# Two engines share the copies of turned attention weights: another split in the third and the fourth batch element

## The chip, the cores and the metric

The kernel runs on one core of a Trainium2 chip. That core has five engines with instruction streams of their own: TensorE (PE, with its weight loads shown apart as PEld), VectorE (DVE), ScalarE (ACT), GpSimd (POOL) and SyncE (SP), whose stream issues the DMAs. Each stream is carried out in the order in which it was built; an instruction that waits for another engine holds up all that stand behind it in its own stream. The metric is the device time of one execution in microseconds (us), and the number to be predicted is the median of several runs.

## The reference

Four batch elements of 512 tokens with 512 channels pass through two blocks. Block 0 is a WKV recurrence over the context and a feed-forward layer (FFN) with quantised activations and one-bit weights. Block 1 is a cross-attention with 16 heads of 32 channels and a last layer with ternary weights. The attention is the part that matters here:

```python
q = _qdq(x) @ _qdq(wq).T + bq
kv = cond @ wkv.T + bkv
k, v = jnp.split(kv, 2, axis=-1)
...
attn = jax.nn.softmax(jnp.einsum('bnhd,bmhd->bhnm', q, k) * scale, axis=-1)
o = jnp.einsum('bhnm,bmhd->bnhd', attn, v).reshape(B, N, C)
out = _qdq(o) @ _qdq(wp).T + bp
```

`attn` must be turned (token axis against key axis) before it can be multiplied with `v` on TensorE. Each turned block appears in PSUM, the accumulators of TensorE, and is copied from there to SBUF, the working memory. The change is about who does that copy.

## The kernel before

The four elements, b = 0 to 3, run as a pipeline. While the FFN of element b+1 runs, the attention of element b fills the gaps, and the WKV part of b+2 beside it. All these parts are Python generators (`ffn_layer`, `attention_layer`, `ternary_layer` and others); `run` takes the next step of the one that is due first, by a place on a time axis that was written out by hand. That fixes TensorE's order through chained dependencies (`in_turn`, `next_turn`). The orders of VectorE and ScalarE are made at build time by a scheduler that estimates when each instruction could run, so moving one instruction from one engine to another can move its neighbours as well.

The attention of one element (`attention_layer`) has 16 units, k = 0 to 15: a unit is one pair of heads, i = 0 and 1, and one half of the queries, which is two tiles of 128, t = 0 and 1. Iteration k of its main loop does, on TensorE and in this order:

- `scores(k, i, 0)`: two score tiles `s_ps`. For each, VectorE takes the negated row maximum, `at_nm` (L962), and ScalarE the exponential, `at_P` (L964). These tiles share three PSUM buffers.
- `values(k-2)`: sixteen small matmuls into `o_ps` from the turned weights `at_PT` of unit k-2; ScalarE copies the result to `at_os` (L1004).
- `turned(k-1, i, 0)`: two groups of four transposes into `pt_ps`, each copied into `at_PT` (L982 by VectorE, L984 by ScalarE).
- `scores(k, i, 1)`, then `turned(k-1, i, 1)`, then `collect(k-2)`: `ot_ps`, divided into `at_o` by VectorE (L1022), with `at_rt` the reciprocal sums (L1020).

So a unit has four copies of turned weights. They are written (k, t, i) below. `at_PT` has one buffer, and `values` starts when all four of its unit are there. In the elements 0 to 2 `pt_ps` shares three PSUM buffers with `o_ps`, `ot_ps`, `qr_ps`, `sx_ps`, `q_ps`; in the fourth element, which the code calls `alone`, `pt_ps` has two buffers of its own, since no FFN runs any more.

```python
dst = PT[k][:, i, :, t * P : (t + 1) * P]
if alone and i:
    made[k] = nc.vector.tensor_copy(dst, blocks(pt))
else:
    made[k] = nc.scalar.copy(dst, blocks(pt))
```

Before its units, an element is prepared in halves of two token tiles. For the fourth element's second half (tiles 2 and 3) this falls among the last units of the third element, once the FFN has written those tiles (`xb`, L788). VectorE computes the layer norm: `BATCH_NORM_STATS2` (L225) and its aggregate (L228), `ln_v`, then about fifteen tiny instructions of a reciprocal square root (`rs_half`, `rs_y`, `rs_t`, L185 to L195), and `ln_r` (L237, L238). GpSimd centres the tiles (`at_xn`, L246), VectorE takes their maxima (`at_s`, L249) and scales (L259, L260), ScalarE rounds (`at_xn`, L264), TensorE turns them (`qr_ps`), ScalarE stores them (`at_xqT`, L271). Then `project(0)` makes the first queries: `q_ps` on TensorE, `at_q` (L912) and `at_half` (L917, L918), a DMA out to `qD` and four DMAs back to `at_qR`, which the first `scores` of the fourth element needs.

Among the first eight units of the fourth element lies the end of the third: `project_out` (`at_o` rounded by ScalarE, `p_ps`, then `at_y` L1058 and `xb` L1059 on VectorE) and the ternary layer, whose statistics, `tf_xn` (L1158) and `tf_s` (L1162 to L1176) are on VectorE, followed by ScalarE's rounding (`tf_xn`, L264), TensorE's `qr_ps` and `f_ps`, and the store (L1190).

Of the kernel before, what the change touches and what calls it, by code (L numbers as in the profile page):

```python
# [30 lines left out]
def kernel(  # L31
# [37 lines left out]
    NB, T, D = x.shape  # L69
# [63 lines left out]
    def psum_tile(name, tag, dtype=F32):  # L133
        pool, bufs = psum["now"]
        return pool.tile([P, D], dtype, name=name, tag=tag, bufs=bufs[tag])
# [34 lines left out]
    def transpose(*args):  # L170
        return in_turn(nc.tensor.transpose(*args))  # L171

    def blocks(a):
        return a.rearrange("p (c q) -> p c q", q=P)
# [680 lines left out]
    def attention_layer(b, xb, pool, tiles=range(NT)):  # L855
# [6 lines left out]
        alone = b == NB - 1  # L862
# [86 lines left out]
        units = [(p, h) for p in range(NP) for h in range(len(tiles) // 2)]  # L949
# [22 lines left out]
        def turned(k, i, t):  # L972

            if k not in PT:
                PT[k] = pool.tile([P, 2, NT, 2 * P], F32, name="at_PT", tag="at_PT", bufs=1)
            w = lanes.pop((k, i, t))
            pt = psum_tile("pt_ps", "acc" if alone else "m")
            for m in range(NT):
                transpose(pt[:, m * P : (m + 1) * P], w[:, m * P : (m + 1) * P], ident)
            dst = PT[k][:, i, :, t * P : (t + 1) * P]  # L980
            if alone and i:
                made[k] = nc.vector.tensor_copy(dst, blocks(pt))  # L982
            else:
                made[k] = nc.scalar.copy(dst, blocks(pt))  # L984
# [99 lines left out]
        for k in range(len(units) + 2):  # L1084
# [8 lines left out]
            for i in range(2):  # L1093
                if before:
                    turned(k - 1, i, 0)
# [8 lines left out]
            for i in range(2):  # L1104
                if before:
                    turned(k - 1, i, 1)
# [331 lines left out]
```

## Time and profile before

| what | value |
|---|---|
| runs | 1122.58, 1123.04, 1125.3 us; median 1123.04 |
| the profiled execution | 1121.98 us; its span 1120.2 us, so 1.78 us lie around the span |
| busy: PE, PEld | 960.3 us (86%), 678.2 us (61%) |
| busy: DVE, ACT, POOL | 886.3 us (79%), 711.5 us (64%), 297.8 us (27%) |
| mean granted TensorE clock | 0.954 |
| copies of turned weights | 224 on ACT, 32 on DVE |

Times inside the profile are microseconds from the start of the span. The shares are means over a pipeline whose stages have different limits; what matters here is the stretch from about 945 to 1040 us, where the third element's attention ends and the fourth's begins. A row of the timeline gives start, duration, engine, line, operation, the tile written and the tiles read, and, in brackets, how long the engine stood idle before it and what released it. VectorE and ScalarE instructions that follow each other overlap a little: two copies of 0.59 us on ACT that start one after the other take 1.07 us together.

### The profile page before, as it was taken

The page shows a single profiled execution, that of the slowest core. Times are in us where ns is not written, and L with a number is a line of the kernel's source. Part 1 is how long each engine was busy: PE and PEld are TensorE (multiplying, and loading weights), DVE is VectorE, ACT ScalarE, POOL GpSimd, SP SyncE. Part 2 cuts the span into 40 slices and gives each one's busy share as a digit, 9 for nine tenths or more (in the row PEclk, how much of TensorE's full clock was granted, in tenths as well). Part 3 has the DMA queues.
Part 4 walks back from the last instruction along what each step waited for, and adds up shares of the span by engine and source line. Part 5 has one row for each costly group of instructions (what it writes and reads, how often), then busy time and mean ns, then how long its engine had stood idle before and what let it go on. Part 6 is the DMA issues. An engine that isn't in the chain of part 4 may idle for free.

```text
span 1120.2 us, 16509 instructions
## 1 busy us (share of the span) xinstructions
PE 960.3 (86%) x5520; PEld 678.2 (61%) x5548; DVE 886.3 (79%) x1884; ACT 711.5 (64%) x1454; POOL 297.8 (27%) x301
## 2 busy tenths in 40 slices
PE   3879898978878978899998797999999899788983
PEld 3345565555546756677776475777777677555651
DVE  5887447778877799998759899977689766689866
ACT  5657655453214677667768676687676677887762
POOL 3822014333104143541215536212122400100000
PEclk8889999998888999999999999999999899999997
DMA  8188953544434664654655555464564563243401
GB/s 281 39 274 321 322 203 129 178 169 153 148 122 151 224 191 157 200 178 163 205 188 184 164 168 181 142 220 157 181 227 156 181 201 110 89 134 109 123 11 38
DMA packets 85668, 189.58 MB, mean 169 GB/s; under 512 B 12240, under 2 KB 36816, under 8 KB 74576
## 3 DMA queue, kind: packets, MB, share of 16 engines
q1 hardware_dynamic: 85584, 188.53, 50.2%
q8 instruction: 44, 0.72, 0.3%
q14 instruction: 40, 0.33, 0.1%
HBM read 148.65 MB, written 39.85 MB: 168 GB/s over the span
## 4 chain that ended last, share of the span: by engine, by line
PE 46%; DVE 28%; ACT 12%; issue 5%; DMA 5%; POOL 3%; SPq 1%; POOLq 0%; ACTq 0%; DVEq 0%
PE ff_hp L168 13%; PE ff_acc L168 6%; PE pt_ps L171 6%; PE o_ps L168 4%; PE v_ps L168 3%; PE s_ps L168 3%; DVE wk_q L655 3%; DVE at_nm L962 3%; ACT at_P L964 3%; PE k_ps L168 2%; PE tp_ps L171 2%; DVE qg_i L695 2%; PE qr_ps L171 1%; ACT at_PT L984 1%; DVE ff_z L765 1%
## 5 line engine op out<-in xcount | busy, mean ns | idle before, releaser
L168 PE MATMUL ff_hp<-wT,xp 128*128 128x512 f32 x1024 | 270.5, 408 | 3.3 <-ACT at_P L964 2.1
L168 PEld LDWEIGHTS ff_hp<-wT,xp 128*128 128x128 f32 x1024 | 194.3, 193 | 51.3 <-ACT at_P L964 4.4
L964 ACT ACTIVATE at_P<-s_ps,at_nm 128x512 f32<-128x512 f32 x256 | 174.5, 689 | 61.8 <-DVE at_nm L962 61.4
L962 DVE TENSOR_REDUCE at_nm<-s_ps 128x1 f32<-128x512 f32 x256 | 166.0, 677 | 28.4 <-PE s_ps L168 28.0
L700 POOL TENSOR_TENSOR ff_z<-qg_b,qg_s 128x512 f32<-128x512 bf16 x64 | 71.1, 1111 | 381.1 <-ACT qg_b L699 328.4
L171 PE MATMUL pt_ps<-ident,at_P 128*128 128x128 f32 x1024 | 141.3, 278 | 11.7 <-ACT at_os L1004 5.2
L984 ACT COPY at_PT<-pt_ps 128x512 f32<-128x512 f32 x224 | 124.7, 595 | 38.1 <-PE pt_ps L171 37.5
L171 PEld LDWEIGHTS pt_ps<-ident,at_P 128*128 128x128 f32 x1024 | 113.2, 141 | 53.1 <-issue 13.8
L168 PE MATMUL ff_acc<-wT,hr 128*128 128x512 f32 x512 | 136.6, 408 | 6.3 <-DVE hr L712 3.3
L168 PE MATMUL s_ps<-at_kR,at_qR 128*128 128x512 f32 x256 | 98.1, 449 | 21.9 <-ACT at_P L964 14.6
L168 PEld LDWEIGHTS ff_acc<-wT,hr 128*128 128x128 f32 x512 | 92.4, 190 | 27.3 <-DVE hr L712 4.6
L760 ACT ACTIVATE ff_z<-ff_hp,coef 128x512 f32<-128x512 f32 x64 | 43.9, 686 | 67.2 <-PE ff_hp L168 65.2
L168 PE MATMUL o_ps<-at_PT,at_V 128*32 128x256 f32 x1024 | 72.0, 395 | 1.3 <-DVE hr L712 0.7
L699 ACT CAST qg_b<-qg_i 128x512 bf16<-128x512 int8 x80 | 49.4, 618 | 36.7 <-DVE qg_i L695 24.6
L168 PE MATMUL v_ps<-wkvT,cT 128*128 128x512 f32 x128 | 65.9, 664 | 5.3 <-DVE wT L336 2.3
L765 DVE SCALAR_TENSOR_TENSOR ff_z<-ff_hp,coef,ff_z 128x512 f32<-128x512 f32 x64 | 47.6, 744 | 27.9 <-PE ff_hp L168 27.8
L168 PEld LDWEIGHTS s_ps<-at_kR,at_qR 128*128 128x128 f32 x256 | 45.7, 193 | 39.4 <-ACT at_P L964 23.8
L761 DVE SCALAR_TENSOR_TENSOR ff_z<-ff_z,ff_hp 128x512 f32<-128x512 f32 x64 | 43.4, 679 | 24.2 <-ACT ff_z L760 24.0
L168 PE MATMUL k_ps<-cT,wkvT 128*128 128x512 f32 x128 | 59.3, 613 | 3.1 <-ACT cT L479 1.4
L711 ACT CAST hr<-tp_ps 128x512 fp32r<-128x512 f32 x64 | 37.6, 587 | 35.7 <-PE tp_ps L171 35.7
L655 DVE RECIPROCAL wk_q<-wk_q 128x256 f32<-128x256 f32 x32 | 54.3, 1718 | 1.4 <-POOL wk_p L643 1.4
L171 PE MATMUL tp_ps<-ident,ff_z 128*128 128x128 f32 x256 | 41.2, 286 | 14.4 <-ACT at_PT L984 5.3
(190 smaller groups left out, 1735.7 us busy)
## 6 DMA issues: line engine op xcount, KB each, us to landing
wT<-wD SPq DMA_DIRECT2D x72, 1024.0 KB, 5.2
wn<-in_L_ffn_w_dram SPq DMA_DIRECT2D x18, 1024.0 KB, 6.8
at_kR<-kD SPq DMA_DIRECT2D x128, 128.0 KB, 3.0
at_qR<-qD SPq DMA_DIRECT2D x256, 64.0 KB, 2.2
wD<-wT SPq DMA_DIRECT2D x12, 1024.0 KB, 5.0
kD<-k_half SPq DMA_DIRECT2D x16, 512.0 KB, 3.3
qD<-at_half SPq DMA_DIRECT2D x32, 256.0 KB, 2.1
cn<-in_ctx_dram SPq DMA_DIRECT2D x8, 512.0 KB, 5.9
```

Of the source, the lines that this page charges most:

```text
L168: return in_turn(nc.tensor.matmul(*args, **kwargs))
L171: return in_turn(nc.tensor.transpose(*args))
L655: nc.vector.reciprocal(half, half)
L699: nc.scalar.copy(qb, qi)
L700: nc.gpsimd.tensor_tensor(grouped(src), grouped(qb), s.unsqueeze(2).to_broadcast([P, NG, GS]), ALU.mult)
L711: nc.scalar.copy(part[:, 0, :], pt)
L760: nc.scalar.activation(z, hp, AF.Tanh, scale=coef[:, 0:1])
L761: nc.vector.scalar_tensor_tensor(z, z, 1.0, hp, ALU.add, ALU.mult)
L765: nc.vector.scalar_tensor_tensor(z, hp, coef[:, 1:2], z, ALU.mult, ALU.mult)
L962: nc.vector.tensor_reduce(nm, sp, AX.X, ALU.max, negate=True)
L964: nc.scalar.activation(lanes[k, i, t], sp, AF.Exp, bias=nm, accum_out=sums[k][:, t, i : i + 1],)
L984: made[k] = nc.scalar.copy(dst, blocks(pt))
```

## The change

The rule for who copies is replaced. In the third element (b = NB - 2) VectorE takes the copies with i = 1 of the units 11 to 15, ten in all, which were ScalarE's. In the fourth element VectorE keeps the copies with i = 1 of the units 8 to 15, and of the units 0 to 7 only the one with t = 1; the eight copies (k, 0, 1) of these units go to ScalarE. VectorE then has 34 copies and ScalarE 222.

```diff
-            if alone and i:
+
+            if alone:
+                share = i and (t or k >= len(units) // 2)
+            else:
+                share = b == NB - 2 and i and k >= len(units) - 5
+            if share:
                 made[k] = nc.vector.tensor_copy(dst, blocks(pt))
             else:
                 made[k] = nc.scalar.copy(dst, blocks(pt))
```

In the built instruction lists TensorE's and GpSimd's orders are the same as before. In SyncE's list one load of `at_kR` for the fourth element moves from before to after a store of the output. VectorE's and ScalarE's lists differ from about 950 us of the profile before until about 1040 us, and not only by the copies themselves.

## The prediction

> **What bounds the kernel now.** I looked first at the copies, then at who waits around them, then at the chain of work that ended last. The view of the tile `at_PT` gives the two prices:
>
> ```profile
> L984 ACT COPY at_PT<-pt_ps x224: 565/592/658, 398.9 to 1082.5; 128x512 f32<-128x512 f32 x112
> L982 DVE COPY at_PT<-pt_ps x32: 670/690/693, 988.5 to 1083.0; 128x512 f32<-128x512 f32 x32
> ```
>
> These are spans of single instructions. In a full queue the next one starts earlier: ScalarE's pairs take 1.07 us, so a copy more costs 0.48 to 0.50, and on VectorE 0.60 (copy at 988.48, next instruction at 989.08). Table of busy time by stretch (length; busy us of PE, PEld, DVE, ACT, POOL; granted clock; DMA):
>
> ```profile
> 952.00:964.00 12.00, 10.64 (x91) 7.71 (x91) 10.12 (x33) 10.36 (x27) 2.22 (x3) 1.00 0.30 88
> 964.00:972.00 8.00, 5.90 (x52) 4.22 (x51) 4.20 (x11) 7.91 (x20) 1.76 (x2) 1.00 0.01 3
> 980.00:985.00 5.00, 4.49 (x26) 2.11 (x28) 3.05 (x7) 3.51 (x8) 0.00 (x0) 0.66 0.56 182
> 1000.00:1020.00 20.00, 18.69 (x156) 12.13 (x147) 19.30 (x40) 13.94 (x36) 0.00 (x0) 1.00 0.35 104
> 1020.00:1031.00 11.00, 7.14 (x56) 4.86 (x54) 11.00 (x39) 8.63 (x22) 0.00 (x0) 1.00 0.49 141
> 1031.00:1040.00 9.00, 8.78 (x65) 5.55 (x70) 8.56 (x27) 7.24 (x16) 0.00 (x0) 0.81 0.04 11
> ```
>
> ScalarE is full where it loses copies (7.91 of 8 us) and VectorE is full where it loses some (19.30 of 20, 11.00 of 11). By these shares both moves look right. But a full engine is not yet the path, so I read the chain that ended last, in the first stretch:
>
> ```profile
> 965.01 0.70 ACT at_xn L264
> ...
> 967.56 0.58 ACT at_xqT L271
> ...
> 972.84 0.61 PE q_ps L168 x2
> 973.54 0.76 DVE at_q L912
> 974.33 0.73 ACT at_half L917
> 975.07 2.03 DMA qD<-at_half
> 978.42 1.90 DMA at_qR<-qD
> 980.46 1.19 PE s_ps L168 x2
> ```
>
> It goes through the preparation of the fourth element's second half: its rounding, its transposes, the queries, the DMAs out and back, the first scores at 980.46. TensorE stands idle for 2.35 us before those. The timeline shows where the preparation comes from and, in the second stretch, the largest stall:
>
> ```profile
> 961.52 0.15 DVE L238 SCALAR_TENSOR_TENSOR ln_r<-mv,rs_y 128x2 f32<-128x2 f32 x1
> 965.76 0.66 PE L171 MATMUL qr_ps<-ident,at_xn 128*128 128x128 f32 x4 [1.23 <-ACT at_xn L264]
> ...
> 1029.94 0.20 DVE L1171 TENSOR_SCALAR tf_s<-tf_s,rs_y 128x1 f32<-128x1 f32 x1
> 1031.05 0.93 PE L171 MATMUL qr_ps<-ident,tf_xn 128*128 128x128 f32 x4 [2.75 <-ACT tf_xn L264]
> ```
>
> **Stage A, the third element's units 11 to 15: ten copies from ScalarE to VectorE.** TensorE's order is unchanged, so the question is what each of its waits now ends on. In VectorE's old list the layer norm's small instructions end (`ln_r`, 961.52 to 961.67) before the maxima of unit 14's second scores. In the new list `ln_r` stands behind five of the ten copies, (11,1,1) to (13,1,1), and behind these two maxima as well. Count from `xb` L788, which the FFN releases at 952.02 in both: 961.67 + 5 copies of 0.60 + 2 maxima of 0.62 = 965.9. I walked the new lists with the durations of these rows, 0.1 to 0.15 us a hand-off. TensorE reaches the end of unit 13's second transposes at 963.15 instead of 964.15, since ScalarE is lighter; copy (13,1,1) starts at 963.9, and a reciprocal `at_rt`, now ahead of the last small steps, waits for unit 14's last exponential until 965.0. `ln_r` ends at 966.35, 4.7 us late.
>
> From there: GpSimd 0.1 + 0.76, the maximum 0.60; the second maximum waits for GpSimd's second tile (1.52 for both), the scales follow both maxima, ScalarE's `at_xn` starts at 969.1 and TensorE's `qr_ps` 0.86 later at 970.0, as in the old rows (964.90, 965.76). That is 4.2 us late. In the old order a maximum of scores stood between these steps, so 0.5 comes back. Behind `qr_ps` TensorE's whole list waits: it has `ot_ps` of unit 12 done at 963.6 and idles 6.4 us instead of 1.23.
>
> From `qr_ps` to `q_ps` it was 965.76 to 972.41, 6.65 us, set by ScalarE. With two copies fewer there and both tiles rounded ahead, the walk gives 6.05. But the stretch now begins after a long idle time, and the rows show what follows: after 2.35 us of idle the granted clock is 0.66 (980 to 985), after 2.75 us `qr_ps` takes 0.93, `s_ps` 0.85 and `o_ps` 1.87 us where they take 0.45, 0.46 and 1.00 at full clock. That is 1.74 us for just the three that follow here, of which 1.4 remains beside ScalarE's work. So `q_ps` starts at 970.0 + 6.05 + 1.4 = 977.45, 5.0 late. `q_ps` to the first scores stays 8.05 us, a chain with two DMA legs in which no copy stands between. ScalarE's relief of 10 x 0.48 = 4.8 us is worth the 1.0 and 0.6 already counted, and nothing more: the copies of unit 15 lie under the 2.35 us of waiting for the DMA. If that cover were gone they would bring 4 x 0.5 - 2 x 0.6 = 0.8.
>
> A = +5.0. Low end: VectorE without a single wait ends `ln_r` at 965.3, and full clock: 3.6 - 0.5 - 0.6 = +2.5. High end: the 0.6 doesn't come and 1.9 us of slow clock: 4.2 + 1.9 = +6.1.
>
> **Stage B, the fourth element's units 0 to 7: eight copies from VectorE to ScalarE.** VectorE loses 8 x 0.60 = 4.8 us, ScalarE gains 8 x 0.48 = 3.8, beside 13.94 busy of 20. Walked from the first scores on, with the old time base: nothing until unit 1 (`values(0)` at 992.0 after 991.8, because the copy (0,1,0) now stands behind two exponentials), 0.75 us ahead at `values(4)`, and none left at `values(5)`, since the new list puts two `tf_xn` ahead of maxima that TensorE's scores wait for. Then the stall: `tf_s` ends at 1028.2 instead of 1030.1, TensorE waits 1.15 us instead of 2.75, `qr_ps` starts at 1029.65, and after an idle time so short the clock stays full (the 1.23 us before 965.76 were followed by normal 0.66). So the 1.74 us of slow clock go too: `values(6)` ends 3.1 ahead. By `values(7)` 2.5 remain, as ScalarE's copy (7,1,0) comes after two exponentials.
>
> [...]
>
> B = -2.5 by the walk. The nearest thing that undoes it is a remaining stall that is longer than the 1.23 us: with the slow clock kept, -2.5 + 1.74 = -0.8. A walk of some forty hand-offs sees only the waits it looks for, so I take the middle, -1.6. Ends: -4.8 (all of VectorE's relief on the path) and +1.5 (three of ScalarE's extra copies on the path, where `s_ps` waits for `at_P`).
>
> The load of `at_kR` that moves behind a store: one issue of 0.4 us, due two units later; hidden, and 0.4 without that cover. The rest of the lists is as before, so what is late at 1040 us is late at the end.
>
> **Sum.** +5.04 - 1.6 = +3.44: 1121.98 + 3.44 = 1125.4 for an execution like the profiled one (span 1123.6 and the same 1.78 around it). The median of the runs is 1.06 above that one: 1126.5.
>
> **Rivals.** (1) B gives what the walk says, or all that VectorE loses: -2.5 to -4.8 with A +5.0 or a little less, so 0 to +2.5, about 1124.5: no change that counts. For it: VectorE is 100% busy from 1020 to 1031. Against: between 1000 and 1020 TensorE is busy for 18.69 of 20 and can give back 1.3 at most. (2) Faster: ScalarE is the bound in stage A (7.91 of 8) and the layer norm isn't. It decides if `ln_r` ends by 962.6, less than 1 us late, so that `qr_ps` still finds its tile. Then three copies of 0.5 before `qr_ps` are won, A = -1.5, and with B = -2.5: -4.0, 1119.0. Against: the new list has `ln_r` behind copy (13,1,1), whose transposes alone end at 963.15. (3) That the change does nothing is excluded by the lists: 34 and 222 copies.
>
> **Numbers.** About 0.3% (3.4 us) is what a measurement of this kernel can tell from no change. Slower by more, the sum or worse: 0.54; within: 0.36; faster: 0.10. The range goes from rival 2 (1119.0, 0.2 of room) to A at +6.1 with B at +1.5 (+7.6, 1130.6).
>
> **What would show it.** Right: `ln_r` L238 about 4 to 5 us later than 961.5; a TensorE stall of 5 to 7 us before the `qr_ps` that waits for `at_xn`, granted clock near 0.66 behind it; the first scores of the fourth element near 985.5; a shorter or vanished stall before the `qr_ps` that waits for `tf_xn`, with full clock. Wrong: first scores at or before 981, or `values(7)` (1039.5 before) under 1039.

## The result, and the profile after

| | before | after |
|---|---|---|
| median of the runs that stand beside each other | 1122.81 us (8 runs, 1119.77 to 1125.3) | 1128.88 us (8 runs, 1127.28 to 1133.59) |
| ratio | | 1.0064, interval 1.0044 to 1.0084 |
| the profiled execution, its span | 1121.98, 1120.2 us | 1127.48, 1125.7 us |
| mean granted clock | 0.954 | 0.948 |

The changed kernel is slower by about 6 us. In the two profiled executions it is 5.5 us. The ratio, here and below, is formed from all runs of both kernels; it is not the ratio of the two medians, which would be 1.0054.

The view of the tile `at_PT`, with minimum, median and maximum duration in ns, shows first that the copies went where the change says:

```profile
L989 ACT COPY at_PT<-pt_ps x222: 572/592/649, 395.6 to 1087.0; 128x512 f32<-128x512 f32 x111
L987 DVE COPY at_PT<-pt_ps x34: 677/691/692, 950.2 to 1087.4; 128x512 f32<-128x512 f32 x34
```

Busy time by stretch, in the columns of the table shown for before (length; PE, PEld, DVE, ACT, POOL; granted clock; DMA):

```profile
952.00:964.00 12.00, 11.37 (x95) 8.09 (x93) 10.74 (x26) 9.01 (x24) 0.00 (x0) 1.00 0.29 88
964.00:972.00 8.00, 2.15 (x11) 1.50 (x13) 4.23 (x21) 3.35 (x8) 3.97 (x4) 0.62 0.01 2
985.00:990.00 5.00, 4.50 (x26) 2.56 (x27) 2.89 (x7) 3.95 (x10) 0.00 (x0) 0.66 0.64 205
1020.00:1031.00 11.00, 9.19 (x76) 5.89 (x76) 10.46 (x34) 8.09 (x22) 0.00 (x0) 1.00 0.60 177
```

From 952 to 964 the move does what it is meant to: ScalarE's busy time falls from 10.36 to 9.01 us, TensorE's rises from 10.64 to 11.37 us. GpSimd, though, falls from 2.22 to nothing: it has no tile to centre yet. The bill comes in the next 8 us. TensorE is busy for 2.15 us where it was 5.90, ScalarE for 3.35 where it was 7.91, and the granted clock is 0.62. All engines wait together, which is what a chain looks like in such a table. The timeline has its links, and the later stalls:

```profile
966.14 0.15 DVE L238 SCALAR_TENSOR_TENSOR ln_r<-mv,rs_y 128x2 f32<-128x2 f32 x1
969.85 1.12 PE L171 MATMUL qr_ps<-ident,at_xn 128*128 128x128 f32 x4 [6.03 <-ACT at_xn L264]
...
1035.73 0.66 PE L171 MATMUL qr_ps<-ident,tf_xn 128*128 128x128 f32 x4 [1.00 <-ACT tf_xn L264]
...
1091.72 1.84 PE L171 MATMUL qr_ps<-ident,at_o 128*128 128x128 f32 x8 [1.30 <-ACT at_o L264]
1093.35 3.05 PE L168 MATMUL p_ps<-wpT,at_oqT 128*128 128x512 bf16 x8
```

`ln_r` is 4.6 us later than before, TensorE's stall ahead of `qr_ps` is 6.03 instead of 1.23 us. The stall before `tf_xn` is 1.00 instead of 2.75, with a normal 0.66 behind it. The chain that ended last, from the rounding to the first scores of the fourth element:

```profile
968.99 0.82 ACT at_xn L264
...
976.80 0.62 PE q_ps L168 x3
...
977.77 0.76 DVE at_q L912
...
978.56 0.73 ACT at_half L917
...
980.09 3.02 DMA qD<-at_half
...
983.48 1.88 DMA at_qR<-qD
...
985.50 0.70 PE s_ps L168 x2
```

The first scores start at 985.50, 5.04 us later than before. Between them and `values(7)` 1.10 us come back; from there to `values(15)` 0.5 is lost. About half of that has a cause in the lists: ScalarE's copy of `values(8)`, `at_os`, stood ahead of two exponentials before and stands behind them now, and TensorE waits 0.71 us for the copy `at_PT` behind it. `values(8)` to `values(9)` is 6.45 us instead of 6.19. It is 6.45 to 6.47 in all kernels below that have the fourth element's part, and at most 6.25 in those that don't. The line is of the changed kernel:

```profile
1052.93 1.09 PE L171 MATMUL pt_ps<-ident,at_P 128*128 128x128 f32 x8 [0.71 <-ACT at_PT L989]
```

The rest, 1.1 us, lies in the last 40 us, where no copy was moved. One part is visible: after the same idle time of 1.30 us, `qr_ps` of `at_o` took 1.38 us before and 1.84 us after. The profile's clock record has the clock at half from 1092.27 to 1095.69 in the changed kernel, and at full until 1099.55 in the kernel before. The line of the kernel before:

```profile
1087.30 1.38 PE L171 MATMUL qr_ps<-ident,at_o 128*128 128x128 f32 x8 [1.30 <-ACT at_o L264]
```

### The profile page after: what moved, and what is told of

It is laid out like the page before. It is cut to its first block, busy times and chain, and to the rows that moved or that the text cites. A ratio compares the mean times of both kernels' runs of the same rounds, so it can differ in the third digit from the quotient of the medians.

```text
span 1125.7 us, 16535 instructions
## 1 busy us (share of the span) xinstructions
PE 964.1 (86%) x5548; PEld 680.9 (60%) x5548; DVE 887.7 (79%) x1886; ACT 710.0 (63%) x1452; POOL 299.0 (27%) x301
## 4 chain that ended last, share of the span: by engine, by line
PE 46%; DVE 26%; ACT 12%; issue 5%; DMA 5%; POOL 4%; SPq 1%; POOLq 0%; ACTq 0%; DVEq 0%
PE ff_hp L168 13%; PE ff_acc L168 6%; PE pt_ps L171 6%; PE o_ps L168 4%; PE s_ps L168 4%; ACT at_P L964 3%; PE v_ps L168 3%; DVE at_nm L962 3%; DVE wk_q L655 3%; PE k_ps L168 2%; DVE qg_i L695 2%; DMA wn<-in_L_ffn_w_dram 2%; PE qr_ps L171 2%; PE tp_ps L171 2%; ACT at_PT L989 2%
## 5 line engine op out<-in xcount | busy, mean ns | idle before, releaser
L168 PE MATMUL ff_acc<-wT,hr 128*128 128x512 f32 x512 | 139.9, 415 | 6.3 <-DVE hr L712 3.3
L168 PEld LDWEIGHTS ff_acc<-wT,hr 128*128 128x128 f32 x512 | 94.7, 194 | 27.9 <-DVE hr L712 4.6
```

The costliest lines, as they stand in the source:

```text
L168: return in_turn(nc.tensor.matmul(*args, **kwargs))
```

## The experiments

Times in this part are counted from the start of the last `xb` (L788) of the FFN. Up to it the lists are the same or nearly so, and yet it starts at 950.1 to 956.6 us in the profiled executions: the mean granted clock up to it is 0.96 in the kernel before and in the changed kernel, which reach it at 952.0 and 952.1, and 0.95 in e12, which reaches it at 954.2. So only stretches counted from a common mark can be compared finely. Each ratio is against runs of the kernel before on the same chip; the milestones are those of one execution of each kernel.

| kernel | `ln_r` | `qr_ps`, stall before it | first scores | `values(0)` | `values(7)` | ratio to before, interval |
|---|---|---|---|---|---|---|
| before | 9.50 | 13.74, 1.23 | 28.44 | 39.78 | 87.50 | |
| after | 14.07 | 17.78, 6.03 | 33.43 | 45.10 | 91.39 | 1.0064, 1.0044 to 1.0084 |
| e1 third element's copies only | 14.06 | 17.78, 6.02 | 34.81 | 47.50 | 95.21 | 1.0071, 1.0045 to 1.0096 |
| e2 fourth element's copies only | 9.51 | 13.75, 1.23 | 28.43 | 41.95 | 88.25 | 0.9991, 0.9977 to 1.0006 |
| e3 four copies instead of ten, third only | 9.50 | 13.74, 1.23 | 28.33 | 39.68 | 87.50 | 1.0000, 0.9984 to 1.0016 |
| e4 change, norm ahead | 11.00 | 15.58, 3.30 | 32.23 | 44.81 | 91.11 | 1.0046, 1.0030 to 1.0062 |
| e5 change, stall filled | 14.05 | 17.77, 1.71 | 32.60 | 43.58 | 89.89 | 1.0045, 1.0024 to 1.0065 |
| e8 = e4 with its stall filled | 11.00 | 15.58, 1.15 | 30.46 | 43.34 | 89.63 | 1.0021, 1.0001 to 1.0041 |
| e12 change, ScalarE padded | 14.06 | 17.78, 6.03 | 32.97 | 46.28 | 92.59 | 1.0028, 1.0004 to 1.0053 |
| e6 before, stall filled | 9.50 | 13.74, 1.23 | 28.63 | 39.59 | 87.40 | 1.0006, 0.9987 to 1.0025 |
| e9 = e2 with its stall filled | 9.50 | 13.74, 1.23 | 28.61 | 39.86 | 86.13 | 0.9990, 0.9973 to 1.0007 |
| e7 before, preparation earlier | 9.31 | 13.03, 2.24 | 30.68 | 42.20 | 89.92 | 1.0022, 1.0001 to 1.0044 |
| e10 = e2, queries earlier | 9.51 | 13.75, 1.23 | 27.89 | 40.06 | 87.82 | 0.9995, 0.9978 to 1.0011 |
| e11 before, queries earlier | 9.51 | 13.75, 1.23 | 27.79 | 39.81 | 86.12 | 0.9992, 0.9974 to 1.0009 |

The theory was that of the prediction: the ten copies push the layer norm back on VectorE, TensorE waits, the slow clock adds to it, and the fourth element's part gives back a little. The rivals were that the loss comes from the fourth element's part, from the copies themselves wherever they stand, or from the clock alone.

### e1 and e2: one part of the change each

```diff
-            if alone and i:
+            if (alone and i) or (b == NB - 2 and i and k >= len(units) - 5):      # e1
+            if alone and i and (t or k >= len(units) // 2):                       # e2
```

> Only the ten copies of the third element go to VectorE; the fourth element stays as before. Theory (VectorE's order puts the layer norm's last step ln_r behind five copies, TensorE's qr_ps waits for it): ln_r near 966.1 instead of 961.5, a TensorE stall of about 6 us before qr_ps, first scores of the fourth element near 985.5, then the second stretch as before, so the whole is later by 5 us or a little more (ratio about 1.0045). Rival (the loss comes from the fourth element, where ScalarE has eight copies more): first scores at most 1 us late and a ratio under 1.001.

> Only the eight copies of the fourth element go to ScalarE; the third stays as before. Theory: ln_r at 961.5 and first scores at 980.5 as before; the stall before the qr_ps that waits for tf_xn shrinks from 2.75 to about 1 us and the slow clock behind it goes, values(7) 1.1 to 2.5 us ahead of 1039.5, the whole 1 to 2.5 us faster (ratio about 0.9985). Rival (ScalarE's eight copies cost more than VectorE's relief): values(7) later than 1039.5 and a ratio of 1.003 or more.

e1 alone has the whole loss: `ln_r` and the stall stand where the full change has them. Its first scores are another 1.4 us later, and later than expected, because the clock stayed at half for longer after the stall: in e1 the granted clock is 0.50 from +17.6 to +23.5, in the changed kernel it is back at full from +20.7. The timeline of TensorE in e1:

```profile
974.23 1.11 PE L171 MATMUL qr_ps<-ident,at_xn 128*128 128x128 f32 x4 [6.02 <-ACT at_xn L264]
...
976.34 1.94 PE L168 MATMUL o_ps<-at_PT,at_V 128*32 128x256 f32 x16
978.20 1.97 PE L171 MATMUL pt_ps<-ident,at_P 128*128 128x128 f32 x8
```

Here `o_ps` takes 1.94 us (1.00 to 1.07 at full clock) and the transposes behind it 1.97; in the changed kernel the transposes were back at 1.09. e2 leaves the layer norm alone, and the ratio holds 1. Its `values(0)` is nevertheless 2.2 us late, and `values(7)`, expected 1.1 to 2.5 us earlier, is 0.75 us later. Busy time by stretch of e2 shows why the comparison of two single executions misleads here:

```profile
985.00:990.00 5.00, 4.87 (x17) 2.91 (x14) 2.27 (x5) 2.85 (x9) 0.00 (x0) 0.50 0.36 107
```

The granted clock is 0.50 in these five microseconds, +30.4 to +35.4 from the mark. In the kernel before it was 0.89 in the same stretch from the mark (982.42 to 987.42), though both had waited the same 2.35 us for the first scores. e9 below takes that difference out.

### e3: a smaller dose

```diff
-            if alone and i:
+            if (alone and i) or (b == NB - 2 and i and k >= len(units) - 2):
```

> As the third-element part alone, but for the units 14 and 15 only: four copies, all of which stand behind ln_r in VectorE's order. Theory: ln_r and the first scores where they were (961.5, 980.5, within 0.4), the whole within 1 us of before (ratio 1.000). Rival (a copy on VectorE is itself the cost, by its 0.1 us more and its share of the engine): four tenths of the loss, first scores near 982.5, ratio near 1.002.

Four copies that stand behind the layer norm in VectorE's list: no milestone moves by more than 0.11 us, and the ratio is 1.0000. So these four copies cost nothing on VectorE in themselves, and win next to nothing either. Whether it is the place ahead of `ln_r` that costs, e4 tells.

### e4 and e8: the layer norm ahead, and its stall filled

In e4 the copies of unit 13 and later, and the maxima of unit 14's second scores, are ordered behind `ln_r` on VectorE. e8 adds ten matmuls, whose result isn't read, in the stall that is left.

```diff
+            if b == NB - 2 and t and k == len(units) - 2:
+                behind(low, norm["last"])
...
+                if not alone and k > len(units) - 4:
+                    behind(made[k], norm["last"])
...
+            if alone and t == 2:          # e8 only
+                filled(10)                # matmuls 128x512 bf16 into an unused bank
             transposed_rows(xqT[:, :, t * P : (t + 1) * P], xn)
```

> The whole change, but the copies of unit 13 and the maxima of unit 14's second scores are ordered behind ln_r on VectorE, by edges that only fix the order; the numbers of copies on each engine are those of the changed kernel. Theory: ln_r near 963.5 (only the copies of the units 11 and 12 are ahead of it now), qr_ps near 967.5, first scores near 982.5 to 983, so 2.5 to 3 us better than the changed kernel and 1 to 2 us worse than before (ratio about 1.0015). Rival (the number of copies on VectorE decides, not their order): as the changed kernel, first scores near 985.5 and ratio 1.005 to 1.006.

> The whole change with the layer norm ahead (as e4), and 10 filling matmuls (2.4 us) in the 3.3 us stall that was left before `qr_ps`. Theory (what e4 still lost behind `qr_ps`, 16.65 us to the first scores where the kernel before takes 14.70, is the slow clock after the stall): `qr_ps` stays at +15.6, first scores at about +30.3 instead of +32.2, ratio about 1.003. Rival (ScalarE's and VectorE's new lists cost those 1.9 us): first scores stay at +32.2, ratio 1.0046.

All ten copies are on VectorE in e4, but only three instead of five come between the mark and `ln_r`, and `ln_r` is 1.5 us late instead of 4.6: the order decides and not the number of copies. For the first scores e4 missed: `qr_ps` is 1.8 us late, the first scores are 3.8 us late. e8 tells what the other 2 us were. First e4, then e8:

```profile
966.13 1.12 PE L171 MATMUL qr_ps<-ident,at_xn 128*128 128x128 f32 x4 [3.30 <-ACT at_xn L268]
...
968.25 1.94 PE L168 MATMUL o_ps<-at_PT,at_V 128*32 128x256 f32 x16
```

```profile
967.19 0.66 PE L171 MATMUL qr_ps<-ident,at_xn 128*128 128x128 f32 x4 [1.15 <-ACT at_xn L268]
...
968.35 1.07 PE L168 MATMUL o_ps<-at_PT,at_V 128*32 128x256 f32 x16
```

`qr_ps` starts at the same +15.58, so nothing became earlier, yet the work behind it, up to the first scores, runs at full clock, and the first scores come at +30.46 instead of +32.23, as the theory had it (about +30.3). The stall of 3.3 us that e4 left cost about as much through the clock (1.8 us) as through the lateness of `qr_ps` (1.8 us). Making `qr_ps` late by less than half as much therefore left three quarters of the loss.

### e5: the change with its stall filled

```diff
+            if alone and t == 2:
+                filled(20)
             transposed_rows(xqT[:, :, t * P : (t + 1) * P], xn)
```

> The whole change, and 20 matmuls of 128x512 bf16 (0.24 us each at full clock, 4.7 us in all, result not read) in TensorE's list ahead of the `qr_ps` that waits 6.03 us for `at_xn`. VectorE, ScalarE and GpSimd keep their lists, so `ln_r` stays 4.5 us late and TensorE keeps an idle stretch of about 1.3 us. Theory (the lateness sets `qr_ps`, and the slow clock after the idle time adds to it): `ln_r` and `qr_ps` where the change has them, +14.1 and +17.8 after the last `xb` of the FFN, full clock behind them, first scores 1.4 us earlier than with the change alone, at about +32.0; time 1.4 us below the change's, ratio about 1.005. Rival (the clock costs nothing, the lateness all): first scores stay at +33.4, ratio 1.0064. Rival (the idle TensorE is only a sign and the slow clock is the whole loss): first scores back at +28.4, ratio 1.001.

The timeline of TensorE:

```profile
971.74 0.66 PE L171 MATMUL qr_ps<-ident,at_xn 128*128 128x128 f32 x4 [1.71 <-ACT at_xn L264]
...
986.57 0.70 PE L168 MATMUL s_ps<-at_kR,at_qR 128*128 128x512 f32 x2 [3.16 <-DMA at_qR<-qD]
987.21 1.07 PE L168 MATMUL o_ps<-at_PT,at_V 128*32 128x256 f32 x16
```

`ln_r` and `qr_ps` stay late to 0.02 us, and the clock stays full. The first scores gain 0.83 us, not the 1.4 that was expected, and most of the change's lateness, 4.2 of 5.0 us, remains: 4.0 from `qr_ps`, 0.7 less up to `q_ps`, and 0.8 more from there on, which e12 looks into. So the lateness is the larger part of the loss and the clock an addition to it. The rival of the clock alone (first scores back at +28.4) is out, and so is the rival that the clock costs nothing. The rest of the gain (`values(0)` 1.5 us earlier than in the change) is an accident of this execution: its 3.16 us wait was followed by full clock (`o_ps` 1.07 us; 1.67 in the change).

### e6 and e9: filling the wait before the first scores

```diff
+                if alone and not k and not i:
+                    filled(8)
                 if now:
                     scores(k, i, 0)
```

> The kernel before, and 8 such matmuls (1.9 us) ahead of the fourth element's first scores, in the 2.35 us that TensorE waits there for the DMA. No other engine's list is changed. Theory (the 0.66 granted after that wait is caused by the idle time and lies on the path): first scores unchanged at +28.4, the next `o_ps` takes 1.1 instead of 1.94 us, `values(0)` about 1.3 us earlier than +39.8, time 1 to 1.5 us lower, ratio 0.999. Rival (other engines hide it): `values(0)` and the time as before, ratio 1.000.

> The fourth element's part of the change alone (as e2), with 8 filling matmuls (1.9 us, result not read) ahead of the fourth element's first scores. Theory (the 2.2 us that e2 was late at `values(0)`, +41.95 where the kernel before has +39.78, are the slow clock that lasted longer after the 2.35 us wait): `values(0)` at about +39.6, the `tf_xn` stall 1.00 us, `values(7)` at about +86.0 instead of 87.5, ratio 0.998 to 0.9985. Rival (it is the wait for ScalarE's copies `at_PT`, more of which now lie there): `values(0)` stays above +41, `values(7)` at +87.5 or later, ratio 1.000.

In e6 the clock behaved as expected, and the time didn't: `o_ps` takes 1.07 instead of 1.94 us, but `values(0)` comes only 0.2 us earlier. First the kernel before, then e6:

```profile
981.58 1.94 PE L168 MATMUL o_ps<-at_PT,at_V 128*32 128x256 f32 x16
```

```profile
985.90 1.07 PE L168 MATMUL o_ps<-at_PT,at_V 128*32 128x256 f32 x16
```

The stretch after the first scores waits for ScalarE's exponentials (1.35 and 1.34 us before a score tile), which hid the slow matmuls in the kernel before, whose clock was at half for 3.41 us, until +31.5. In e2, where it was 0.50 up to +35.4, they weren't hidden. e3 says the same without any filling: its clock happened to stay full after the same wait (2.36 us), and from the first scores to `values(0)` it took 11.35 us, where the kernel before took 11.34. The rival was right here, and my reading of the slow clock in the kernel before as a loss on the path was wrong.

e9 is the fourth element's part with that disturbance out of the way:

```profile
983.50 0.70 PE L168 MATMUL s_ps<-at_kR,at_qR 128*128 128x512 f32 x2 [1.01 <-DMA at_qR<-qD]
...
994.75 1.07 PE L168 MATMUL o_ps<-at_PT,at_V 128*32 128x256 f32 x16 [1.22 <-ACT at_PT L990]
...
1033.30 0.66 PE L171 MATMUL qr_ps<-ident,tf_xn 128*128 128x128 f32 x4 [1.00 <-ACT tf_xn L264]
```

`values(0)` is 0.1 us later than before, since the 1.22 us wait for ScalarE's copies eats what full clock gives; then the `tf_xn` stall falls from 2.75 to 1.00 us, and `values(7)` is 1.4 us earlier. From the first scores to `values(7)` it is 57.52 us, against 59.06 before. The ratio, 0.9990, agrees with about 1.1 us but doesn't tell it from nothing.

### e7, e10 and e11: the preparation earlier

e7 plans the four steps that prepare the second half of the fourth element half a slot (half a unit) earlier; e10 and e11 do it for the first two steps after them, a fifth of a slot, on top of e2 and of the kernel before.

```diff
-            (b + 1 + 1.7 / SLOTS, b + 1 + 3.7 / SLOTS, 4),
+            (b + 1 + 1.2 / SLOTS, b + 1 + 3.2 / SLOTS, 4)      # e7, for b == NB - 1 only
...
-            (b + 1 + 3.75 / SLOTS, b + 1 + 4.35 / SLOTS, 2),
+            (b + 1 + 3.55 / SLOTS, b + 1 + 4.15 / SLOTS, 2),   # e10, e11, for b == NB - 1 only
```

> The kernel before, with the four steps that prepare the second half of the fourth element planned half a unit earlier. TensorE's list has the two `qr_ps` of this half one group of transposes earlier each. Theory (the preparation is the path to the first scores): `ln_r` about +8.7 instead of +9.5, the second `qr_ps` some 2 us earlier, first scores 1.5 to 2 us earlier at about +26.7, time 1.5 to 2.5 us lower, ratio 0.998. Rival (TensorE's list in order: what waits for `at_xn` holds up the third element's scores and exponentials): a stall of 2 to 3 us before the first `qr_ps`, first scores at +28 or later, ratio 1.000 to 1.002.

> The fourth element's part of the change alone, with the fourth element's first two steps after its preparation (query projections, fetches of keys, values, queries) planned a fifth of a slot earlier, so that the first `q_ps` stands ahead of the third element's last second transposes (14,.,1). Theory (the chain preparation, projection, two DMA legs is the path to the first scores): `q_ps` 1.0 us earlier, first scores at about +27.5, the stall before them 1.3 us and then full clock, `values(0)` about +38.6, `values(7)` about +85, ratio 0.9975. Rival (ScalarE's queue takes it back, `at_half` behind two exponentials): first scores +28.2, ratio 0.999 to 1.000.

> The kernel before, with the same two steps a fifth of a slot earlier and no copy moved. Theory: first scores at about +27.5, values(0) 1.0 to 1.4 us earlier than +39.8, the `tf_xn` stall of 2.75 us stays, ratio 0.9988. Rival: ScalarE's queue takes it back, first scores +28.2, ratio 1.000.

e7 went the rival's way. Its two `qr_ps` start 0.7 and 1.0 us earlier, but TensorE now waits 2.24 us for them with the third element's work queued behind:

```profile
963.12 0.66 PE L171 MATMUL qr_ps<-ident,at_xn 128*128 128x128 f32 x4 [2.24 <-ACT at_xn L264]
...
964.54 1.91 PE L171 MATMUL pt_ps<-ident,at_P 128*128 128x128 f32 x8
```

The transposes behind it run at half clock (1.91 us; 1.09 at full), and `q_ps`, which kept its place, comes at +22.7 instead of +20.4; the first scores are 2.2 us late. In e10 and e11 the first scores come 0.55 and 0.65 us earlier, a little more than half of what I had expected, and `values(0)` comes no earlier than before. In e11 the `tf_xn` stall, which was to stay at 2.75 us, is 1.90; the gain of 1.4 us at `values(7)` is down to 0.6 at `values(15)`. None of the runs is a version that can be told from the kernel before as faster.

### e12: is it an instruction load that lengthens the store?

The chain of the changed kernel has one leg that the prediction left unchanged: the second store `qD<-at_half` took 3.0 us to land instead of 2.0. All of after, e1, e4, e5 and e8 show 3.0 to 3.1, and none of the kernels without the ten copies does. In the former a transfer of the queue that the profile calls instruction (q14, one packet) falls within the store. e12 pads ScalarE's list by ten one-column copies, to bring its count of instructions to where it was.

```diff
+            if b == NB - 2 and i and t and k < 10:
+                nc.scalar.copy(sm.tile([P, 1], F32, name="pad", tag="pad"), w[:, 0:1])
```

> The whole change, and ten more one-column copies on ScalarE, one in each of the third element's units 0 to 9 (result not used), so that from there on ScalarE has issued as many instructions as in the kernel before. No other engine's list differs from the change's. In question are the 0.8 us by which `q_ps` to the first scores takes longer with the ten copies (8.86 instead of 8.05 us): the second store `qD` took 3.0 instead of 2.0 us there, and a transfer of queue q14, kind instruction, falls within it in these kernels and in none without the ten copies. Theory (that transfer is ScalarE's instruction load, due at a count of instructions, and it holds up the store): the transfer comes some 10 us earlier against the last `xb`, the store takes 2.0 us, first scores at about +32.6 instead of +33.4. Rival (it belongs to another engine, or has nothing to do with the store): store 3.0 us, first scores at +33.4 or later. The ratio, 1.0057 or 1.0064, can't tell them apart.

SyncE's waits (total, times, longest) in the changed kernel, then in e12:

```profile
SPq L927 <- DMA qD<-at_half: 1.3, 2, 0.9
```

```profile
SPq L927 <- DMA qD<-at_half: 0.3, 1, 0.3
```

The wait for the store is back at the 0.3 us of before, the first scores come 0.46 of the 0.8 us earlier, and no instruction transfer lies within the store any more. But the transfer didn't move to the place that I had given it: it comes at +30.6, after the store, instead of +29.9, so it is not shown to be ScalarE's. One of the four loads `at_qR` that follow took 0.79 us to issue (0.43 at most before), which is where the other 0.3 went. So the store's extra microsecond came and went with ten instructions on another engine. That the instruction load is the cause is not shown, and one observation speaks against it: in the kernel before, a transfer of the same queue (+28.8) falls within a later store `qD` (issued at +28.6), which took 2.03 us. It began 0.2 us after that store's issue, and 1.8 to 1.9 us after it in the slow cases, so only its place within the store could make the difference. The cause stays open. The ratio of e12, 1.0028, overlaps with the change's, and its milestones behind the first scores are no better.

## Why the prediction was right, point by point

The outcome, slower by over 0.3%, was the likeliest case, and 1128.88 us lies within the range, 2.4 us above the single figure. Its steps:

**`ln_r` late behind five copies and two maxima: right.** Predicted end 966.35, measured 966.29 (966.14 + 0.15). e1, e3 (no copy ahead of `ln_r`, 0.0 us late) and e4 (three, 1.5 us) show that this is the cause.

**`qr_ps` at 970.0 after a 6.4 us stall: right.** 969.85 after 6.03 us.

**`qr_ps` to `q_ps`, 6.05 us at full clock and 1.4 us for the slow clock: the first right, the second mis-sized.** e5 has 5.98 us at full clock; the changed kernel takes 6.79, so the slow clock cost 0.81. The prediction took the 1.74 us of three slow instructions and, for this execution, hid too little of it. In e1 the same stall cost about 1.4 us more (8.22 us from `qr_ps` to `q_ps`), because the clock came back later (after +23.5, not at +20.7): the size of this term varies from one execution to the next, and one value in a sum hides that.

**`q_ps` to the first scores, unchanged 8.05 us: failed.** It is 8.86 in the changed kernel and 8.85 in e5, so it isn't the clock; it is the store's third microsecond (3.02 us to land instead of 2.03). "A chain with two DMA legs in which no copy stands between" was true of the instructions and not of the DMA legs' durations. What came before was 0.15 us (`qr_ps`) and 0.66 us (`qr_ps` to `q_ps`) earlier than predicted, this leg 0.81 us longer. They cancel, and the first scores stood at 985.50 exactly as predicted. That is luck: an end that agrees does not show that its terms do.

**Stage B, -1.6, between the walk's -2.5 and less: right in kind, the walk itself too large by 1.0 to 1.4 us.** Measured -1.1 there and -1.5 in e9. The `tf_xn` stall is 1.00 us instead of the predicted 1.15, with full clock behind it. What the walk didn't see is the loss at the start: the 1.22 us wait of `values(0)` for ScalarE's copies, for which the walk had 0.2 us of lateness. At `values(4)`, where it had 0.75 us of lead over the first scores, the changed kernel is 0.17 behind and e9 0.26 ahead. That -1.6 came close is owed to the allowance for waits not seen, not to the walk.

**"What is late at 1040 us is late at the end": short by 1.6 us.** From `values(7)` to `values(15)` the changed kernel needs 44.26 us instead of 43.78: the lists differ a little beyond 1040 us, and the displaced `at_os` costs 0.26 of this, in every kernel with the fourth element's part. The other 1.1 us are in the tail, with a clock that was at half at other times in the two executions. The sum of +3.4 against the measured +5.5 of the two profiled executions is this, and B's half microsecond.

**Slow clock behind the long stall, full clock behind the short one: right here, but the length alone doesn't settle it.** `qr_ps` took 1.12 us behind the 6.03 us and 0.66 behind the 1.00 us. In the kernel before the granted clock was 0.66 from 980 to 985, with the wait of 2.35 us ahead, and 0.57 from 1031 to 1035, behind the 2.75 us. But e7 shows half clock after a stall of 2.24 us, and e5 ran on at full clock after 3.16, so no shortest stall explains both. The last section has what the clock records of the two kernels show.

**The rivals.** B giving back all of A didn't happen: TensorE, at 18.69 of 20 us busy, had little to return. ScalarE as the bound of stage A fell with the first step, since `ln_r` ended at 966.29 and not by 962.6. What ScalarE's relief is worth shows in e5, where `qr_ps` to `q_ps` took 5.98 us instead of 6.65: the 0.6 of the sum, and no more. e3 adds little, as only one of its four copies falls in the 8 us in which ScalarE was full (7.58 busy there instead of 7.91); `q_ps` comes 0.1 us earlier.

## What to carry to other kernels

When work moves to an engine whose busy share looks lower, look for the small instructions in its list that feed a chain, and count what the move puts ahead of them: here a reciprocal square root, a dozen instructions of 0.13 to 0.17 us each, held up a five-engine chain by 4.6 us because five copies and two maxima came ahead of its steps or between them. An engine that is full in a stretch isn't the bound unless what it feeds is late; read the chain first, then the shares. And when a delay is repaired by half, look at the granted clock behind the idle time that is left: the 3.30 us that e4 left cost 1.8 us through the clock, as much as the lateness of `qr_ps`.

## What the runs showed of the hardware

- **The same idle time was followed by full clock and by half.** Normal times followed waits of 1.00 and 1.22 us (e9, `qr_ps` 0.66 and `o_ps` 1.07), 1.15 (e8), 1.23 (the kernel before) and 1.71 us (e5; `qr_ps` 0.66 in all three). Slow ones followed, at once or 1.4 us later, after 2.24 (e7, `pt_ps` 1.91), 3.30 (e4, `qr_ps` 1.12) and 6.03 us (the changed kernel, `qr_ps` 1.12). But after 2.35 us the clock fell to 0.50 in the kernel before, and in e3 it stayed at 1.00 after 2.36; after 2.75 us `qr_ps` took 0.93 in the kernel before, after 2.76 it took 0.66 in e1, and after 3.16 us `o_ps` took 1.67 in the changed kernel and 1.07 in e5. After the 1.30 us ahead of `qr_ps` of `at_o` the clock was at full for another 12.2 us in the kernel before, and at half 0.6 us later in the changed kernel.
- **The stretches at half clock began whole multiples of 3.413 us after each other, and not at a fixed place of a stall.** The clock records of the kernel before (19 such stretches) and of the changed kernel (22) show it; but for the last of each record, the stretches also lasted whole multiples, 3.41 to 13.65 and 3.41 to 17.07 us. In the changed kernel one began 2.15 us into the 6.03 us stall and one 0.55 us after the end of the 1.30 us stall ahead of `at_o`, in the kernel before one began 0.23 us after the end of the 2.75 us stall. The 2.35 us before the first scores, in successive intervals of 3.41 us; the columns are those of the tables above (length; PE, PEld, DVE, ACT, POOL; granted clock; DMA). First the kernel before, then e3, which has the same TensorE list:

```profile
976.67:980.08 3.41, 1.43 (x12) 1.29 (x12) 1.92 (x7) 2.15 (x4) 0.00 (x0) 1.00 0.69 209
980.08:983.49 3.41, 3.03 (x19) 1.14 (x19) 1.95 (x5) 2.77 (x6) 0.00 (x0) 0.50 0.59 197
```

```profile
976.55:979.96 3.41, 1.98 (x16) 1.61 (x15) 2.91 (x6) 1.76 (x3) 0.00 (x0) 1.00 0.72 239
979.96:983.37 3.41, 2.13 (x19) 0.90 (x19) 3.00 (x9) 1.92 (x3) 0.00 (x0) 1.00 0.58 205
983.37:986.78 3.41, 2.66 (x15) 1.84 (x16) 2.09 (x4) 2.54 (x9) 0.00 (x0) 1.00 0.47 143
```

Idle time of 1.98 us in one such interval was followed by half clock, 1.43 and 1.28 us in two were not. With the two records cut into intervals of this length from the first stretch at half on, each of the 21 drops from 400 us to the end of the last whole interval followed an interval with at least 1.83 us idle, and every interval at full clock with more than 1.91 us idle was followed by a drop; between the two it went either way.
- **How long it stayed low varied too:** 3.41 us after 2.35 us of waiting in the kernel before, and 6.83 us after the 6.03 us stall in the changed kernel. After the same two waits it was low for longer in e2 (0.50 up to +35.4, against +31.5 in the kernel before) and in e1 (0.50 up to +23.5, against +20.7 in the changed kernel). With it `values(0)` came 2.2 us late in e2, and 0.1 us late in e9, whose stall is filled: a difference as large as what was studied here.
- **A 256 KB store to DRAM took 2.0 or 3.0 us** at the same place in the same queue order, consistently by kernel (2.03 us in the kernel before, 3.02 in the changed kernel), and changed with ten tiny instructions on another engine (e12: the longest wait for it 0.3 us instead of 0.9). Why is open.
